# Layer 1 of a two-layer network: the state updated by one multiply-add on VectorE for each pair, the inverses begun three pieces later, and the quantised weight prepared behind the first block

## The chip, the core and the metric

The kernel runs on one NeuronCore of a Trainium2 chip. TensorE (PE) multiplies matrices, VectorE (DVE), ScalarE (ACT) and GpSimd (POOL) work on elements, and the transfers are issued from SyncE's queue (SP). The metric is device time of one launch in microseconds. Less is better. Three runs of the kernel before gave 3066.98, 3079.79 and 3086.23 us, so the median is 3079.79 us.

## What is computed

The input is one sequence of 4096 rows with 256 channels. Layer 0 (causal attention with 16 heads, then a mixture of experts) is not touched by the change. Layer 1 is a delta rule in chunks of 32 rows for 4 heads of 64 channels, followed by a multiplication with an int8 weight. Cut to what matters here, it computes:

```python
h = _layernorm(x) * (1 + ca) + sa
q, k, v = short_conv(h @ Wq, conv_q), short_conv(h @ Wk, conv_k), short_conv(h @ Wv, conv_v)
q, k = l2norm(rotary_mix(q)), l2norm(rotary_mix(k))
kb = k * beta[..., None]
gm = gamma.reshape(b, h, n, chunk).mean(-1)        # one number for a chunk and head
A = -(kb @ swapaxes(k, -1, -2)) * strict_lower      # 32 x 32 for each chunk and head
for i in range(1, chunk):                           # T = inverse of I - A
    A = A.at[..., i, :i].add(einsum('...j,...jc->...c', A[..., i, :i], A[..., :i, :i]))
T = A + eye(chunk)
u, w = T @ v, T @ kb

def step(S, xs):                                    # one chunk of 32 rows
    qi, ki, ui, wi, g = xs
    attn = qi @ swapaxes(ki, -1, -2) * tril_inc
    u_t = ui - wi @ S
    o_i = qi @ S + attn @ u_t
    S_new = g[..., None, None] * S + einsum('bhck,bhcv->bhkv', ki, u_t)
    return S_new, o_i
# ... o normed, times Wo, plus a gated mixer; x = x + ga * that
h = _layernorm(x) * (1 + cb) + sb
# round(h / scale) as int8 @ weight_q.T * scale * weight_scale + bias;  x = x + gb * that
```

The 128 steps of the scan follow each other: each needs the S of the one before.

## The kernel before

Layer 1 works on 8 blocks of 512 rows, each of four tiles of 128 rows. A tile has four chunks. `layer1` (from L1143) runs two streams of generators, `fronts` and `backs`. A piece is what a stream issues up to its next `yield`.

The front (`fronts`, L1266) norms and projects a block (`project`, nine pieces), and then for each tile convolves, rotates and normalises (`convolve`, `mix`), turns keys by channel (`keys_by_channel`) and builds the products of keys (`products`, L1555). `products` scales the products on ScalarE into a tile L, sends L and the betas to DRAM with four transfers each (L1576, L1578), and reads them back with two as Ls (L1581), where each partition has one 32 x 32 matrix. After a block's fourth tile, `solve` (L1585) starts the inverses of its 64 chunk and head pairs at once: GpSimd clears a tile T, ScalarE copies the diagonal from Ls (L1593), and VectorE then works through 31 columns with a multiply and a subtract each (`column`, L1603 and L1610). The last column sends T to DRAM and back as U (18 transfers). These columns are not issued at once. `begin` fills a list of them, and `solving(n)` hands out n of them wherever it is called.

The back (`backs`, L1639) runs the scan and what follows from it. `from_inverse` multiplies U with v and the keys into u and w, `scan` (L1677) does the four steps of a tile, and `weights`, `outputs` and ten further functions make the output of a tile, each a fixed number of pieces later. A step of the scan (L1683 to L1727) is: four TensorE products w @ S (eight matmul instructions) into the PSUM tile w (`pw`), two ScalarE operations that scale the old S by gm into a tile gs (L1694), four columns of an inverse, VectorE's ut = u - w @ S (L1699), one or two yields, TensorE's keys times ut into other columns of the same PSUM tile, three columns, and VectorE's S = gs + that (L1722). The PSUM tile has one buffer. A tile's `weights` hands out two more columns, so a tile takes 30 of the 31.

Three things set the order. First, `layer1` calls the streams: front alone, with three columns after each piece, until the first block's inverse has been issued (`alone(0)`), then `LEAD` = 18 front pieces, then 0.7 front pieces (`RATE`) for each back piece. Before a block's first `from_inverse`, `alone(b)` would run the front on if its inverse were missing. Second, `later(n, f)` has f issued n steps of its stream later (`stream`, L1185). A quiet f adds no piece. When a stream has ended, what waits is issued with no steps between, one piece for each f that is not quiet. Third, instructions issued through `self.mm`, `self.mma`, `self.tp` and `self.dv` (and `keep_in_program_order`) keep their order on their engine. ScalarE's and GpSimd's instructions and the transfers are not pinned: the framework orders those at compile time by what it takes to be ready. On each engine the final order is fixed, and an instruction that waits holds back all behind it.

In `layer1_weights` (L1209) the int8 weight is loaded as int32 words into a tile with gs's name, cast to bf16 on VectorE (L1252), transposed with four TensorE operations (L1257) and copied from PSUM by VectorE (L1260) into `wqT`. All of this is issued ahead of the first block's work. Its first use is `multiplied`, 17 pieces behind the first scanned tile.

Of the kernel before, what the change touches and what calls it, by code (L numbers as in the profile page):

```python
# [9 lines left out]
BF16 = mybir.dt.bfloat16  # L10
I8 = mybir.dt.int8
I32 = mybir.dt.int32
AF = mybir.ActivationFunctionType
ALU = mybir.AluOpType
# [3 lines left out]
P = 128  # L18
S = 4096
C = 256  # L20
# [76 lines left out]
class _Net:  # L97
# [1111 lines left out]
    def layer1_weights(self):  # L1209
        nc, a, wp = self.nc, self.a, self.wp  # L1210
        m = self.mods[1]
        w = self.w = {}
        w["masks"] = self.t(wp, [P, D_N], "masks")
        nc.sync.dma_start(out=w["masks"], in_=a["const_delta"])
        w["bg"] = self.t(wp, [P, 2, 9], "bg")
        for src, lo, hi in (("Wb", 0, 4), ("Wgamma", 4, 8), ("frac_gate_w", 8, 9)):
            nc.sync.dma_start(
                out=w["bg"][:, :, lo:hi], in_=a["L1_attn_" + src].rearrange("(k p) n -> p k n", p=P)
            )
        w["bgb"] = self.t(wp, [P, 9], "bgb")  # L1220
        nc.vector.memset(w["bgb"], 0.0)
        nc.sync.dma_start(out=w["bgb"][:, 8:9], in_=a["L1_attn_frac_gate_b"].partition_broadcast(P))

        w["ones"] = self.t(wp, [P, P], "ones")
        nc.gpsimd.memset(w["ones"], 1.0)


        rl = self.rows(wp, a["L1_attn_rot_logit"], 4, "rl")
        w["mix"] = self.t(wp, [P, 4], "mix")
        nc.scalar.activation(w["mix"], rl, AF.Sigmoid)  # L1230
        w["unmix"] = self.t(wp, [P, 4], "unmix")
        nc.vector.tensor_scalar(w["unmix"], w["mix"], -1.0, 1.0, ALU.mult, ALU.add)


        w["o"] = self.weight(wp, a["L1_attn_Wo"], C, "Wo")
        onw = self.t(wp, [P, 1], "onw")
        for half in range(2):
            nc.sync.dma_start(
                out=onw[64 * half : 64 * half + 64, :],
                in_=a["L1_attn_o_norm_w"].rearrange("(d o) -> d o", o=1),  # L1240
            )
        for k in range(2):
            nc.vector.tensor_scalar(w["o"][:, k, :], w["o"][:, k, :], onw, None, ALU.mult)
            nc.vector.tensor_tensor(w["o"][:, k, :], w["o"][:, k, :], m["ga"], ALU.mult)
        w["gmw"] = self.rows(wp, a["L1_attn_mixer_norm_w"], C, "gmw")
        nc.vector.tensor_tensor(w["gmw"], w["gmw"], m["ga"], ALU.mult)


        words = self.t(self.sp, [P, 2, C // 4], "gs", I32)
        nc.sync.dma_start(out=words, in_=a["L1_ffn_weight_q"].rearrange("(k p) n -> p k n", p=P))  # L1250
        wb = self.t(self.sp, [P, 2, C], "on", BF16)
        nc.vector.tensor_copy(wb, words[:, :, :].bitcast(I8))  # L1252
        w["qT"] = self.t(wp, [P, 2, C], "wqT", BF16)
        for k in range(2):
            ps = self.t(self.pf, [P, C], "f", BF16)
            for ok in range(2):
                nc.tensor.transpose(  # L1257
                    ps[:, ok * P : (ok + 1) * P], wb[:, ok, k * P : (k + 1) * P], self.identb
                )
            nc.vector.tensor_copy(w["qT"][:, k, :], ps)  # L1260
        w["wsg"] = self.rows(wp, a["L1_ffn_weight_scale"], C, "wsg")
        nc.vector.tensor_tensor(w["wsg"], w["wsg"], m["gb"], ALU.mult)
        w["bgo"] = self.rows(wp, a["L1_ffn_bias"], C, "bgo")
        nc.vector.tensor_tensor(w["bgo"], w["bgo"], m["gb"], ALU.mult)

    def fronts(self, later):  # L1266
        nc = self.nc
        for f in self.norm_block(0):
            f()
        yield from self.project(0, later)  # L1270
        for b in range(NB):
            more = b + 1 < NB
            for s in range(4):
                n = 4 * b + s
                parts = self.mix(b, s, later)
                for kinds in (("q", "k"), ("v",), ()):
                    if s in (0, 2):
                        for kind in kinds:
                            yield from self.convolve(s // 2, kind)
                    next(parts)  # L1280
                    yield None
                later(3, lambda n=n: self.keys_by_channel(n))
                later(4, lambda n=n: self.products(n, later))
                if s == 1 and more:
                    self.load_block(b + 1)
                    for at, f in zip((1, 3, 5, 7), self.norm_block(b + 1)):
                        later(at, f, quiet=True)
            if more:
                nc.gpsimd.tensor_copy(self.hT[:, :, 0:8], self.hT[:, :, 512:520])
                for rows in self.shifted:  # L1290
                    nc.gpsimd.tensor_copy(rows[:, :, :, 0:2], rows[:, :, :, 512:514])
                yield from self.project(b + 1, later)
# [292 lines left out]
    def solve(self, b, later):  # L1585


        nc, sp, Ls = self.nc, self.sp, self.Ls
        T = self.t(sp, [P, 16, 32], "T", bufs=1)
        nc.gpsimd.memset(T, 0.0)  # L1590
        for e in range(2):
            half = slice(64 * e, 64 * e + 64)
            nc.scalar.copy(  # L1593
                T[half].rearrange("p m r -> p (m r)")[:, e : e + 34 * 15 + 1 : 34],
                Ls[half].rearrange("p i j -> p (i j)")[:, 33 * e : 33 * e + 66 * 15 + 1 : 66],
            )

        def column(j):
            m, n = j // 2 + 1, 31 - j
            step = self.t(sp, [P, 16, 32], "step", bufs=1)  # L1600
            below = T[:, 0:m, j + 1 : 32]
            self.dv(
                nc.vector.tensor_tensor(  # L1603
                    step[:, 0:m, 0:n],
                    T[:, 0:m, j].unsqueeze(2).to_broadcast([P, m, n]),
                    Ls[:, j + 1 : 32, j].unsqueeze(1).to_broadcast([P, m, n]),
                    ALU.mult,
                )
            )
            self.dv(nc.vector.tensor_tensor(below, below, step[:, 0:m, 0:n], ALU.subtract))  # L1610

        def last():
            column(30)
            dU = self.t(self.dp, [4, 4, 4, 32, 32], "dU")
            for e in range(2):
                nc.sync.dma_start(
                    out=dU.rearrange("t c h (m e) r -> (t c h) m e r", e=2)[:, :, e, :],
                    in_=T[64 * e : 64 * e + 64],
                )
            for t in range(4):  # L1620
                for c in range(4):
                    at = slice(32 * c, 32 * c + 32)
                    nc.sync.dma_start(
                        out=self.U[(4 * b + t) % 6][at, :, at], in_=dU[t, c].rearrange("h j r -> j h r")
                    )
            self.solved += 1

        def begin():
            self.columns = [lambda j=j: column(j) for j in range(30)] + [last]

        later(4, begin, quiet=True)

    def solving(self, n=2):

# [42 lines left out]
    def scan(self, n, later):  # L1677

        nc, sp, kept = self.nc, self.sp, self.tiles[n]
        u, wT, gm = kept["u"], kept["w"], self.blocks[n // 4]["gm"][:, n % 4]  # L1680
        kept["states"] = []
        kept["ut"] = ut = self.t(sp, [P, 4, 64], "ut")
        for c in range(4):  # L1683
            rows = slice(32 * c, 32 * c + 32)
            state = self.state
            kept["states"].append(state)
            pw = self.t(self.pw, [P, 2, 512], "w")
            for pair in range(2):
                for par in range(2):
                    half = slice(64 * par, 64 * par + 64)  # L1690
                    self.mm(pw[rows, par, 64 * pair : 64 * pair + 64], wT[half, pair, rows], state[half, pair, :])
            gs = self.t(sp, [P, 2, 64], "gs")
            for pair in range(2):
                nc.scalar.activation(  # L1694
                    gs[:, pair, :], state[:, pair, :], AF.Identity, scale=gm[:, pair, c : c + 1]
                )
            self.solving(4)
            self.dv(
                nc.vector.tensor_tensor(  # L1699
# [11 lines left out]
            for pair in range(2):  # L1711
                for par in range(2):
# [5 lines left out]
                    )  # L1718
            self.state = self.t(sp, [P, 2, 64], "S", bufs=7)
            self.solving(3)  # L1720
            self.dv(
                nc.vector.tensor_tensor(  # L1722
                    self.state, gs, pw[:, 0, 128:256].rearrange("p (a d) -> p a d", d=64), ALU.add
                )
            )
            yield None

    def weights(self, n):
# [191 lines left out]
```

## Time and profile before

The profiled execution took 3067.4 us, and its span on the core is 3065.6 us; that is the low end of the three timed runs.

| What | Value |
|---|---|
| median of three runs | 3079.79 us |
| profiled execution, its span | 3067.4 us, 3065.6 us |
| granted TensorE clock, mean of the span | 0.912 |
| first loads of layer 1, first scan step | 2102, 2244 us |
| end of the front's matmuls | 2909 us |
| gs, 128x64 on ScalarE (L1694) | 256 times, 343 ns, 77.1 us |
| S, 128x128 on VectorE (L1722) | 128 times, 285 ns, 36.5 us |
| ut, 32x256 on VectorE (L1699) | 128 times, 416 ns, 53.3 us |
| columns, multiply and subtract (L1603, L1610) | 248 each, 315 and 272 ns |
| z, 128x256 multiply-multiply from PSUM on VectorE (L1873) | 32 times, 478 ns |

How to read the lines that follow in the prediction: a row of a timeline has the start and the duration in microseconds, the engine, the source line, the operation, the tile written and the tiles read, and in square brackets how long the engine was idle before it and which instruction ended that. L136, L1329 and L1338 are the helpers through which TensorE's work is issued, so the tile's name tells which it is: w is the scan's PSUM tile, f the front's and other PSUM tiles, o the output's. A row of windows has the window, then for each engine its busy time and number of instructions, and at the end the granted TensorE clock (1 is full speed), the share of the transfer engines and GB/s. A row of the list of waits has who waited for whom, the total in microseconds, how often, and the longest.

### The profile page before, as it was taken

The numbers are of one execution on the slowest core, as the hardware profiler recorded it, in microseconds if no ns is written. First come the engines' busy times: TensorE is split into PE (matmuls) and PEld (weight loads), VectorE is DVE, ScalarE is ACT, GpSimd is POOL, SyncE is SP. The second block draws the span as 40 slices with busy tenths as digits, with TensorE's granted clock in tenths as the row PEclk, the third lists the DMA queues.
The fourth block names the chain that finished last, engine by engine and source line by source line (L and its number), as shares of the span: only waits on it lengthen the run. The fifth ranks groups of instructions, "written<-read, shape, count | busy, mean of one in ns | idle before, by whom it ended". The sixth has DMA issues, their size and how long they took to land. (4 is left out here: it accounts for less than half of the span.)

```text
span 3065.6 us, 60519 instructions
## 1 busy us (share of the span) xinstructions
PE 2807.8 (92%) x24188; PEld 1603.6 (52%) x24188; DVE 2248.7 (73%) x3893; ACT 1814.6 (59%) x3831; POOL 473.1 (15%) x710
## 2 busy tenths in 40 slices
PE   7899999999999999999999899998688889889867
PEld 4454444444444444444444478886466566666545
DVE  6685988888888988989886266665447765765765
ACT  3335777777777787777888632223555455455411
POOL 3232000000000000000000121212324323333312
PEclk8897999999999999999999999998878877778855
DMA  5343000030000300001000100002221212112110
GB/s 187 134 178 66 12 12 7 12 53 7 12 12 7 53 7 12 12 19 38 7 2 2 40 27 28 21 15 80 37 37 27 47 37 43 30 43 41 18 18 11
DMA packets 175083, 111.23 MB, mean 36 GB/s; under 512 B 124177, under 2 KB 143377, under 8 KB 174225
## 3 DMA queue, kind: packets, MB, share of 16 engines
q1 hardware_dynamic: 174656, 107.28, 14.0%
q8 instruction: 191, 3.13, 0.4%
q14 instruction: 92, 0.75, 0.1%
q0 software_dynamic: 144, 0.07, 0.0%
HBM read 54.99 MB, written 37.81 MB: 30 GB/s over the span
## 5 line engine op out<-in xcount | busy, mean ns | idle before, releaser
L723 ACT ACTIVATE e<-e 128x512 f32<-128x512 f32 (+1 forms) x2176 | 1151.4, 583 | 318.7 <-PE e L136 285.1
L605 DVE TENSOR_REDUCE mx<-m 128x2 f32<-128x1024 f32 (+3 forms) x1088 | 1201.7, 1129 | 141.8 <-PE m L136 129.6
L136 PE MATMUL o<-e,vall 128*32 128x256 f32 (+2 forms) x9216 | 692.5, 375 | 6.2 <-ACT ot L700 5.4
L136 PE MATMUL e<-q,kt 50*128 50x512 f32 (+3 forms) x2688 | 573.0, 438 | 1.1 <-ACT e L723 1.0
L136 PE MATMUL m<-kt,q 48*128 48x512 f32 (+3 forms) x2688 | 478.0, 374 | 18.2 <-DVE mx L615 10.7
L136 PEld LDWEIGHTS e<-q,kt 50*128 50x128 f32 x2688 | 251.0, 185 | 433.4 <-issue 258.4
L136 PEld LDWEIGHTS o<-e,vall 128*32 128x32 f32 x9216 | 191.9, 108 | 325.8 <-issue 299.8
L136 PEld LDWEIGHTS m<-kt,q 48*128 48x128 f32 x2688 | 248.7, 189 | 91.9 <-issue 37.1
L1338 PE MATMUL b<-w,hid 128*128 128x512 f32 x768 | 198.0, 402 | 0.0
L902 POOL TENSOR_TENSOR full<-full,ga 128x512 f32<-128x512 f32 (+1 forms) x2 | 2.0, 1001 | 1115.1 <-DMA full<-in_L_attn_bo_dram 1102.8
L1127 DVE SCALAR_TENSOR_TENSOR x<-b,wd,x 128x256 f32<-128x256 f32 x256 | 123.5, 482 | 58.3 <-PE b L1338 51.3
L1338 PEld LDWEIGHTS b<-w,hid 128*128 128x128 f32 x768 | 143.9, 189 | 31.0 <-ACT hid L881 0.3
L1694 ACT ACTIVATE gs<-S,gm 128x64 f32<-128x64 f32 x256 | 77.1, 343 | 113.8 <-DVE S L1722 113.4
L136 PE MATMUL w<-S,uw 64*32 64x64 f32 x1024 | 66.8, 265 | 72.6 <-DVE S L1722 71.7
L1603 DVE TENSOR_TENSOR step<-T,Ls 128x126 f32<-128x126 f32 (+22 forms) x248 | 78.2, 315 | 70.8 <-ACT T L1593 32.8
L615 DVE TENSOR_REDUCE mx<-m 128x8 f32<-128x1024 f32 x64 | 78.4, 1225 | 64.0 <-PE m L136 63.7
L1699 DVE TENSOR_TENSOR ut<-uw,w 32x256 f32<-32x256 f32 x128 | 53.3, 416 | 84.1 <-PE w L136 82.6
L1338 PE MATMUL a<-hs,kt 128*128 128x512 f32 x384 | 104.0, 410 | 1.0 <-DVE hid L1077 1.0
L1722 DVE TENSOR_TENSOR S<-gs,w 128x128 f32<-128x128 f32 x128 | 36.5, 285 | 88.1 <-PE w L136 51.0
L136 PEld LDWEIGHTS w<-S,uw 64*32 64x32 f32 x1024 | 41.2, 129 | 113.3 <-DVE S L1722 95.8
L136 PE MATMUL w<-ut,kk 32*64 32x64 f32 x1024 | 69.8, 267 | 22.2 <-DVE ut L1699 22.1
L1338 PE MATMUL f<-hh,wqkv 128*128 128x512 f32 x288 | 87.4, 448 | 1.4 <-ACT rowsk L1373 0.9
(309 smaller groups left out, 3692.7 us busy)
## 6 DMA issues: line engine op xcount, KB each, us to landing
q<-qd SPq DMA_DIRECT2D x128, 96.0 KB
kt<-kd SPq DMA_DIRECT2D x12, 768.0 KB
kd<-high SPq DMA_DIRECT2D x32, 256.0 KB
qd<-high SPq DMA_DIRECT2D x32, 256.0 KB
x<-in_L_attn_x_dram SPq DMA_DIRECT2D x15, 512.0 KB
kd<-full SPq DMA_DIRECT2D x16, 256.0 KB
qd<-full SPq DMA_DIRECT2D x16, 256.0 KB
xd<-x SPq DMA_DIRECT2D x8, 512.0 KB
```

Of the source, the lines that this page charges most:

```text
L136: self.nc.tensor.matmul(out, lhsT, rhs, start=start, stop=True, skip_group_check=skip)
L605: nc.vector.tensor_reduce(mx[:, 2 * pair : 2 * pair + 2, s, col], ps[:, :, at : at + w], AX.X, ALU.max)
L615: nc.vector.tensor_reduce(mx[:, 2 * pair : 2 * pair + 2, :, 0], ps.rearrange("p h (s k) -> p h s k", k=P), AX.X, ALU.max,)
L723: nc.scalar.activation(e[:, 0:at], ps[:, 0:at], AF.Exp)
L902: nc.gpsimd.tensor_tensor(wide, wide, by.unsqueeze(1).to_broadcast([P, *shape]), op)
L1127: nc.vector.scalar_tensor_tensor(x, ps[:, e, :], wd[:, s, n : n + 1], x, ALU.mult, ALU.add)
L1338: self.nc.tensor.matmul(out, lhsT, rhs, start=(k == 0), stop=(k == n - 1))
L1603: nc.vector.tensor_tensor(step[:, 0:m, 0:n], T[:, 0:m, j].unsqueeze(2).to_broadcast([P, m, n]), Ls[:, j + 1 : 32, j].unsqueeze(1).to_broad ...
L1694: nc.scalar.activation(gs[:, pair, :], state[:, pair, :], AF.Identity, scale=gm[:, pair, c : c + 1])
L1699: nc.vector.tensor_tensor(ut[rows].rearrange("p (a b) d -> p a b d", b=2), u[rows].rearrange("p (a b) d -> p a b d", b=2), pw[rows, :, 0:1 ...
L1722: nc.vector.tensor_tensor(self.state, gs, pw[:, 0, 128:256].rearrange("p (a d) -> p a d", d=64), ALU.add)
```

## The change

The scaling on ScalarE and the tile gs are gone. The new S is made by two VectorE instructions, one for each pair of heads, as old S times gm plus the PSUM columns of the pair. `begin` is issued seven steps after `solve` in place of four. The quantised weight's load, cast, transposes and copies move out of `layer1_weights` into a function of their own, which the front calls behind the first block's projection; it is one front piece more. Its cast, transposes and copies are now pinned to program order, and its words lie in a tile with z's name.

```diff
@@ layer1_weights
-        words = self.t(self.sp, [P, 2, C // 4], "gs", I32)
-        nc.sync.dma_start(out=words, in_=a["L1_ffn_weight_q"].rearrange("(k p) n -> p k n", p=P))
-        wb = self.t(self.sp, [P, 2, C], "on", BF16)
-        nc.vector.tensor_copy(wb, words[:, :, :].bitcast(I8))
-        w["qT"] = self.t(wp, [P, 2, C], "wqT", BF16)
-        for k in range(2):
-            ps = self.t(self.pf, [P, C], "f", BF16)
-            for ok in range(2):
-                nc.tensor.transpose(
-                    ps[:, ok * P : (ok + 1) * P], wb[:, ok, k * P : (k + 1) * P], self.identb
-                )
-            nc.vector.tensor_copy(w["qT"][:, k, :], ps)
...
+    def quantised_weight(self):
+        nc, a, wp = self.nc, self.a, self.wp
+
+        words = self.t(self.sp, [P, 2, C // 4], "z", I32, bufs=1)
+        nc.sync.dma_start(out=words, in_=a["L1_ffn_weight_q"].rearrange("(k p) n -> p k n", p=P))
+        wb = self.t(self.sp, [P, 2, C], "on", BF16)
+        self.dv(nc.vector.tensor_copy(wb, words[:, :, :].bitcast(I8)))
+        self.w["qT"] = self.t(wp, [P, 2, C], "wqT", BF16)
+        for k in range(2):
+            ps = self.t(self.pf, [P, C], "f", BF16)
+            for ok in range(2):
+                self.tp(ps[:, ok * P : (ok + 1) * P], wb[:, ok, k * P : (k + 1) * P], self.identb)
+            self.dv(nc.vector.tensor_copy(self.w["qT"][:, k, :], ps))
...
@@ fronts
         yield from self.project(0, later)
+        self.quantised_weight()
+        yield None
...
@@ solve
-        later(4, begin, quiet=True)
+        later(7, begin, quiet=True)
...
@@ scan
-            gs = self.t(sp, [P, 2, 64], "gs")
-            for pair in range(2):
-                nc.scalar.activation(
-                    gs[:, pair, :], state[:, pair, :], AF.Identity, scale=gm[:, pair, c : c + 1]
-                )
...
             self.state = self.t(sp, [P, 2, 64], "S", bufs=7)
             self.solving(3)
-            self.dv(
-                nc.vector.tensor_tensor(
-                    self.state, gs, pw[:, 0, 128:256].rearrange("p (a d) -> p a d", d=64), ALU.add
-                )
-            )
+            for pair in range(2):
+                self.dv(
+                    nc.vector.scalar_tensor_tensor(
+                        self.state[:, pair, :],
+                        state[:, pair, :],
+                        gm[:, pair, c : c + 1],
+                        pw[:, 0, 128 + 64 * pair : 192 + 64 * pair],
+                        ALU.mult,
+                        ALU.add,
+                    )
+                )
             yield None
```

## The prediction

> **What bounds the kernel now.** I first read the page's header and its slices for the share of layer 1, then layer 1 in windows, then the timelines of VectorE and TensorE in one block, and the list of waits last, because it can name the wrong engine.
>
> ```profile
> span 3065.6 us, 60519 instructions
> PE 2807.8 (92%) x24188; PEld 1603.6 (52%) x24188; DVE 2248.7 (73%) x3893; ACT 1814.6 (59%) x3831; POOL 473.1 (15%) x710
> PEclk8897999999999999999999999998878877778855
> ```
>
> Layer 1 is the last 960 us: its first loads are issued at 2102 and the first scan step runs at 2244. The granted clock is already below 1 there. The windows below hold a whole block of 512 rows (blocks repeat every 112.8 us), then the stretch with the columns of an inverse, then the rest.
>
> ```profile
> 2382.50:2495.30 112.80, 96.37 (x909) 70.58 (x907) 73.71 (x204) 62.14 (x170) 37.13 (x69) 0.85 0.23 45
> 2489.80:2535.50 45.70, 35.10 (x302) 24.91 (x300) 36.70 (x109) 18.29 (x51) 12.84 (x27) 0.77 0.17 40
> 2535.50:2602.60 67.10, 62.25 (x564) 46.12 (x565) 36.54 (x95) 39.51 (x111) 24.01 (x41) 0.78 0.19 35
> ```
>
> In the rest TensorE is busy 62.25 of 67.1 us (93%) and bounds. In the column stretch it is idle 10.6 of 45.7 us, and VectorE bounds: it first stands still, then runs almost without a gap. VectorE there, then TensorE:
>
> ```profile
> 2486.70 0.29 DVE L1722 TENSOR_TENSOR S<-gs,w 128x128 f32<-128x128 f32 x1 [2.49 <-ACT rowsk L1373]
> 2489.40 0.43 DVE L1699 TENSOR_TENSOR ut<-uw,w 32x256 f32<-32x256 f32 x1 [2.42 <-PE w L136]
> 2495.32 0.21 DVE L1603 TENSOR_TENSOR step<-T,Ls 128x31 f32<-128x31 f32 x1 [5.49 <-ACT T L1593]
> 2496.86 0.29 DVE L1722 TENSOR_TENSOR S<-gs,w 128x128 f32<-128x128 f32 x1
> ```
>
> ```profile
> 2486.14 0.45 PE L136 MATMUL w<-ut,kk 32*64 32x64 f32 x8
> 2497.20 0.62 PE L136 MATMUL w<-S,uw 64*32 64x64 f32 x8 [2.66 <-DVE S L1722]
> 2505.88 0.32 PE L136 MATMUL w<-S,uw 64*32 64x64 f32 x2 [3.65 <-DVE S L1722]
> 2537.22 1.97 PE L136 MATMUL o<-ut,A 128*128 128x64 f32 x8
> 2564.95 1.10 PE L136 MATMUL o<-ut,A 128*128 128x64 f32 x8
> ```
>
> The first column waits 5.49 us for T, which ScalarE fills from Ls when that transfer lands. The scan's S is queued behind it, and TensorE waits for S.
>
> ```profile
> ACT gs L1694 <- DVE S L1722: 113.4, 63, 7.1
> DVE step L1603 <- ACT T L1593: 32.8, 6, 5.5
> DVE step L1603 <- DMA Ls<-dL: 32.0, 2, 19.7
> ```
>
> So six such stalls make 32.8 us, and the first and the last block have 19.7 and 12.3 us. The page also puts about 36 us of S's waits down to ScalarE. That is a trap: at 2486.70 the named rowsk has just ended, but so have the w matmuls that S reads (2486.14 + 0.45). Only 2.9 us (five times 0.58) are waits for gs itself. Taking gs away doesn't make S earlier.
>
> **The change, part by part.** The sum is against the profiled execution, 3067.4 us (span 3065.6). The median shown is 3079.8, 0.4% above it; I move the median by the same difference.
>
> *Inverses.* Counting yields in the code, `begin` (L1628) lands at the same place of the scan in blocks 1 to 6, before S of the last chunk of the block's second tile, because VectorE's columns are handed out by the scan. What moves is the front: the first scan step must await the first inverse, so all front work is three pieces (four with the quantised weight's) earlier against the scan. From `products` of a block's last tile to its `begin` there are then 13 pieces of the scan side, not 9. A block is 60 such pieces, 1.88 us each, so Ls is asked for 7.5 us earlier. That covers 5.5 us: 6 x 5.5 = **-33 us**. The front's transfers (24 of rows a block, ten for each `products`) move with it and keep their order on SP's queue; they pass only the scan's stores, one a tile. On GpSimd's queue the front's operations pass the scan's powers and adds, about 1 us each; GpSimd is busy 37.13 of 112.8 us, so I count nothing.
>
> What is late next is VectorE itself. At tile 11's first `ut`, just behind the last column, it has done the same front work in both orders, so the stall is gained whole there; but TensorE has 1.3 us less work in the stretch (keys and products 1.5, a convolution 1.1 come in; a projection 1.65 and two convolutions 2.2 go out), and has it in the rest, where it bounds: 6 x 1.3 = **+8 us**. In the last block `begin` follows `products` with no piece between, before and after, since the stream is drained there: the 12.3 us stay.
>
> In the first block `turning` comes after 9 columns, not 18. TensorE waits there 5.5 us for rot and 5.7 for kk, both behind columns; that shortens by some 6 us. The columns end some 4 us later (one more tile's rotation lies between), and with them U's transfers (16 issues, 8.4 us). TensorE reaches the first inverse's products 8.8 us after the last U is issued (2242.1, 2233.3), so I put this at **0**, between -6 and +6. The front's lead at the end is worth four pieces at the tail's pace in place of the block's, 15.6/15 = 1.04 against 1.88: **-3.4 us**.
>
> *State.* Out go 256 ScalarE scalings (343 ns, 77 us busy) and 128 adds of VectorE (128x128, 285 ns). In come 256 multiply-adds, 128x64, which no row shows. The nearest is z (L1873), also from PSUM with a scalar per row: 478 ns at 256 columns. S at 128 and ut at 256 columns (285, 416) give 1.02 ns a column, so at 64 columns 478 - 192 x 1.02 = 282 ns. How two follow each other:
>
> ```profile
> 2988.97 0.29 DVE L1722 TENSOR_TENSOR S<-gs,w 128x128 f32<-128x128 f32 x1 [0.40 <-PE w L136]
> 2989.17 0.16 DVE L1848 RECIPROCAL rq<-xs 128x1 f32<-128x1 f32 x1
> ```
>
> The next starts 0.20 us after S. The pair takes 0.20 + 0.28 = 0.48 us against 0.285: **+0.2 us** a chunk. The Trainium skill, "VectorE: DVE Perf Modes", the section on the errata, speaks against this edit: each instruction pays its fixed price, so many small tiles pay it many times. Its formula for an fp32 tensor_tensor, (N + 151)/0.96 ns, gives 291 at 128 (the row says 285) and 224 at 64: +0.16 a chunk. I take the trace's 0.2. The bounds are 0.1 and, if nothing shrinks with width, 2 x 0.478 - 0.085 - 0.285 = 0.6.
>
> No overlap of the halves helps: tile w has one buffer, so the next chunk's matmuls wait for both. Where TensorE has other matmuls to do after a chunk (half a microsecond and more), 0.2 is hidden. It shows in the column stretch (5 chunks a block) and where TensorE waits for S in the rest (3 a block): 8 x 6 x 0.2 = 9.6 us. In the tail 2.5 chunks of each of nine tiles are on the chain: 4.5 us. Sum **+14 us**; if the cover were gone everywhere, 128 x 0.2 = 26 us.
>
> ScalarE waits at gs for S 113 us, but the operations behind it (convk, on, uw at 2502, 2509 and 2517) wait for TensorE anyway. I credit one wait, TensorE for mixer (1.35 us a block at 2532.5), with the 0.6 us that one pair of gs takes: **-3.6 us**.
>
> *Quantised weight.*
>
> ```profile
> 2109.29 2.07 ACT L1322 ACTIVATE nxn<-x,nnm,nrs 128x256 f32<-128x256 f32 x4
> 2112.65 0.59 PE L1257 MATMUL f<-identb,on 128*128 128x128 bf16 x4 [10.59 <-DMA bgo<-in_L_ffn_bias_dram]
> 2113.03 1.91 PE L1329 MATMUL f<-k,nxn 128*128 128x128 f32 x8
> ```
>
> nxn is complete at 2111.4, but its transposes are queued behind the weight's until 2113.0: -1.6 us. The four transposes come back behind the projection: +0.6. The cast (0.43 us) and two copies (0.28 each) fall in VectorE's 15 us wait for qk (2119 to 2134). **-1.0 us.** That supposes the transfer to be issued early. It has no input to wait for, and the table trig, also written behind the projection's first pieces, is issued at 2109.6. SP's queue then loses one issue (0.39 us) ahead of wsg and bgo. Were it issued behind the rows at 2131.5 (3.7 us from issue to cast), the first convolution on TensorE and `turning` on VectorE would queue behind it: +7 us.
>
> Sum: -33 + 8 + 0 - 3.4 + 14 - 3.6 - 1 = **-19 us**: 3048 for the profiled execution, 3061 as a median.
>
> **The rivals.** *TensorE's clock stays up* (0.32). Fewer gaps may spare half-speed stretches. The trace: after the stall's window (TensorE busy 0.76 of 3.42 us) the clock is 0.5 most of the time to 2521, and again from 2535 to 2555, where `o<-ut,A` takes 1.97 us against 1.10. The Trainium skill, "TensorE: Matmul & The Clock Gate", part 1, says that about 3.4 us of idleness halve the clock; here gaps of 2.66 and 1.35 us were enough, so by the rule only the stall counts and by the trace smaller gaps do too. The stretch at 2535 lies where TensorE bounds and costs 20 x (1 - 1.10/1.97) = about 9 us. If half to all of the six blocks lose it: -19 - 27 to -54, 3034 to 3007. Against it: the gaps of the column stretch remain, and one of them can throttle as before.
>
> *The pair is dear* (0.10; the other side). At 0.6 us a pair the 70 exposed chunks cost 41 us, not 14, and the 58 others are no longer covered by half a microsecond of TensorE; with half of those, +17. Sum -19 + 27 + 17 = +25, and with all 128 exposed, -33 + 77 = +44: 3105 to 3124. It decides from 33/128 = 0.26 us a pair if all are exposed, 0.47 if 70 are. For it: S is the loop's own chain, and VectorE has no gap in the column stretch. Against: ut and S do shrink with width.
>
> *The stall only changes its name* (0.08). `turning` reaches VectorE's queue nine columns earlier and may wait for qk, and the weight's transfer may come late: -19 + 15 + 7 = +3, 3083.
>
> **How the numbers follow.** My sum has 0.50; with its bounds (first block 6 us either way, S 7 us less or 12 more, the stall's cover a few us) it spans 3045 to 3076. One per cent, about what a measurement of this kernel can tell from no change, is 3049 to 3111. Faster by more: the clock's case and the low end of mine (0.08), 0.40. Slower by more: most of the dear pair, 0.08. Within: 0.52. The range leaves out the clock's best end and the dear pair: 3020 to 3090.
>
> **What would show it.** Right: the first column in blocks 1 to 6 waits under 1 us for T; the last block still about 12; blocks under 110 us; multiply-adds of about 0.28 us, 0.48 a pair; S still named as waiting for TensorE; the nxn transposes start at once behind nxn. Wrong: a column stretch as long as before with another wait in it, pairs of 0.6 us and more, or half-clock windows that come or go.

## The result, and the profile after

The changed kernel takes 3092.9 us (median of 20 runs) against 3077.8 us for the kernel before, timed beside it: ratio 1.0052, interval 1.0033 to 1.0072. It is half a per cent slower. Forecast were 3061 us in a range of 3020 to 3090, with slower by over 1% at 0.08; the direction was wrong, and the time lies just above the range. Medians are over all runs and ratios over the fast runs alone, so a ratio is not always that of two medians.

The page of the changed kernel: the span, the busy times, and the granted clock in 40 slices.

```profile
span 3101.1 us, 60445 instructions
PE 2824.2 (91%) x24188; PEld 1616.5 (52%) x24188; DVE 2268.9 (73%) x4021; ACT 1750.2 (56%) x3575; POOL 472.5 (15%) x710
PEclk8895999999999999999999899998888878778855
```

Not all of the 35.5 us between the two spans belongs to the change. Layer 0 is the same in both programs, yet the first load of layer 1 is issued at 2115.41 us here and at 2102.13 before. So I measure layer 1 from that issue to the end of the span: 963.5 us before, 985.7 after, **+22.2 us**. All "layer 1" times below are taken so, from one profiled execution each. Two kernels were profiled twice, and their layer 1 differs by 0.8 us (e4, e12) and 3.3 us (e7, e13), while its first load comes anywhere from 2101 to 2146 us in the 14 traces. ScalarE lost 64 us of work, VectorE gained 20, and the layer became longer.

The windows are the third block, from its first column to the fourth's, and then the fourth in two parts: from the start of its first column's wait the stretch with the columns, and the rest up to the next wait (length, busy time and instructions of PE, PEld, DVE, ACT and POOL, then granted clock, transfer share, GB/s).

```profile
2409.45:2522.50 113.05, 93.85 (x862) 70.02 (x862) 75.80 (x220) 50.05 (x130) 36.40 (x68) 0.80 0.19 37
2516.90:2562.60 45.70, 32.48 (x254) 24.43 (x250) 34.68 (x106) 12.18 (x35) 11.39 (x23) 0.73 0.09 21
2562.60:2629.20 66.60, 60.34 (x612) 44.40 (x612) 41.13 (x113) 37.76 (x95) 25.27 (x45) 0.90 0.26 49
```

The two blocks take 113.0 and 112.3 us. Before, the same two took 105.9 and 112.8:

```profile
2389.41:2495.32 105.91, 90.24 (x862) 67.05 (x862) 73.28 (x203) 57.40 (x162) 36.94 (x68) 0.84 0.20 40
2495.32:2608.14 112.82, 97.36 (x862) 71.05 (x862) 73.26 (x204) 57.81 (x162) 36.85 (x68) 0.77 0.19 37
```

So the kernel before has two kinds of block. Its 862 matmul instructions, with the same stall of 5.49 us, take 90.2 us of TensorE at a granted clock of 0.84 and 97.4 us at 0.77. The 112.8 us that the prediction takes for every block is of the longer kind: from the second block's first column to the seventh's the intervals are 105.0, 105.9, 112.8, 113.1 and 109.4 us before, and 110.7, 113.0, 112.3, 112.9 and 112.8 after.

Where the 22.2 us lie: up to the third block's first column layer 1 takes 294.0 us (287.3 before), from there to the last block's first column 538.9 (533.4), from there to the end 152.8 (142.9). The gain expected of the blocks is missing, and all three parts are longer. VectorE's timeline shows why: the wait of the first column is still there.

```profile
2513.71 0.47 DVE L1721 SCALAR_TENSOR_TENSOR S<-S,gm,w 128x64 f32<-128x64 f32 x2 [2.52 <-PE w L136]
2516.45 0.43 DVE L1697 TENSOR_TENSOR ut<-uw,w 32x256 f32<-32x256 f32 x1 [2.27 <-PE w L136]
2522.49 0.21 DVE L1606 TENSOR_TENSOR step<-T,Ls 128x31 f32<-128x31 f32 x1 [5.61 <-ACT T L1596]
2524.27 0.47 DVE L1721 SCALAR_TENSOR_TENSOR S<-S,gm,w 128x64 f32<-128x64 f32 x2
```

And the list of waits over the span has the two rows of the first column as before, hardly changed (32.8 and 32.0 us there). TensorE's wait for S is longer (71.7 us there):

```profile
PE w L136 <- DVE S L1721: 86.9, 41, 4.9
DVE step L1606 <- ACT T L1596: 33.3, 6, 5.6
DVE step L1606 <- DMA Ls<-dL: 30.1, 2, 19.5
```

Yet Ls is asked for earlier. Its two transfers are issued from 2511.79, 5.1 us ahead of the wait's start; before, from 2488.81, 1.0 us ahead. The reason is in ScalarE's timeline, which shows its queue in order; first before, then after:

```profile
2494.59 0.60 ACT L1432 ACTIVATE convq<-f 128x512 f32<-128x512 f32 x1 [0.99 <-PE f L136]
2495.08 0.45 ACT L1593 COPY T<-Ls 64x16 f32<-64x16 f32 x2
```

```profile
2515.47 1.28 ACT L1435 ACT_TABLE_LOAD   x1
2516.76 0.60 ACT L1435 ACTIVATE convq<-f 128x512 f32<-128x512 f32 x1
2519.18 0.60 ACT L1435 ACTIVATE convk<-f 128x512 f32<-128x512 f32 x1 [1.82 <-PE f L136]
2520.74 0.58 ACT L1451 COPY qk<-f 128x512 f32<-128x512 f32 x1 [0.97 <-PE f L1332]
2521.36 0.98 ACT L1460 ACTIVATE rot<-qk,unmix 128x128 f32<-128x128 f32 x3
2522.25 0.20 ACT L1596 COPY T<-Ls 64x16 f32<-64x16 f32 x1
2522.36 0.40 ACT L1460 ACTIVATE rot<-qk,unmix 128x128 f32<-128x128 f32 x1
2522.78 0.22 ACT L1596 COPY T<-Ls 64x16 f32<-64x16 f32 x1
```

The two copies that fill T now stand behind both convolutions, the copy qk and the rotations of the next block, which themselves wait for TensorE. Before, they stood directly behind convq. Nobody wrote this order: these instructions aren't pinned. The chain that ended last agrees; between 2516 and 2530 us it runs over the front's matmuls, qk and rot to T's copies, the columns and S, and no transfer is in it. Some of its pieces (start, duration, what):

```profile
2518.12 1.01 PE f L136 x8
2519.13 1.06 PE f L1341 x4
2520.19 0.45 PE f L1332 x4
2520.74 0.59 ACT qk L1451
2521.67 0.68 ACT rot L1460 x2
2522.78 0.23 ACT T L1596
2524.27 0.47 DVE S L1721 x2
```

So two theories had to be told apart. *Queue*: the change is slow because T's copies slid back in ScalarE's queue. *Pair*: the two multiply-adds lengthen the chain of S by more than the sum allowed for.

### The profile page after: what moved, and what is told of

Read it like the earlier page. It is cut to its first block, busy times and chain, and to the rows that moved or that the text cites. A ratio compares the mean times of both kernels' runs of the same rounds, so it can differ in the third digit from the quotient of the medians.

```text
span 3101.1 us, 60445 instructions
## 1 busy us (share of the span) xinstructions
PE 2824.2 (91%) x24188; PEld 1616.5 (52%) x24188; DVE 2268.9 (73%) x4021; ACT 1750.2 (56%) x3575; POOL 472.5 (15%) x710
## 4 chain that ended last, share of the span: by engine, by line
PE 65%; DVE 24%; ACT 5%; issue 3%; POOL 2%; DMA 1%; SPq 0%; DVEq 0%; ACTq 0%; POOLq 0%
PE o L136 16%; PE e L136 13%; DVE mx L605 9%; PE m L136 8%; PE b L1341 6%; PE f L1341 5%; PE f L136 5%; PE a L1341 4%; PE w L136 3%; DVE step L1606 2%; DVE T L1613 2%; PE ps L1341 2%; ACT e L723 1%; PE f L1332 1%; DVE S L1721 1%
## 5 line engine op out<-in xcount | busy, mean ns | idle before, releaser
L136 PE MATMUL m<-kt,q 48*128 48x512 f32 (+3 forms) x2688 | 480.9, 376 | 15.3 <-DVE mx L615 9.0
L1606 DVE TENSOR_TENSOR step<-T,Ls 128x126 f32<-128x126 f32 (+22 forms) x248 | 78.5, 317 | 69.5 <-ACT T L1596 33.3
L1721 DVE SCALAR_TENSOR_TENSOR S<-S,gm,w 128x64 f32<-128x64 f32 x256 | 60.2, 276 | 87.7 <-PE w L136 86.1
L136 PE MATMUL f<-frac,hT 128*128 128x128 f32 x640 | 94.9, 304 | 0.0
```

The source lines that it names most:

```text
L136: self.nc.tensor.matmul(out, lhsT, rhs, start=start, stop=True, skip_group_check=skip)
L1606: nc.vector.tensor_tensor(step[:, 0:m, 0:n], T[:, 0:m, j].unsqueeze(2).to_broadcast([P, m, n]), Ls[:, j + 1 : 32, j].unsqueeze(1).to_broad ...
L1721: nc.vector.scalar_tensor_tensor(self.state[:, pair, :], state[:, pair, :], gm[:, pair, c : c + 1], pw[:, 0, 128 + 64 * pair : 192 + 64 * ...
```

## The experiments

Each kernel was timed in five rounds against the kernel before, and its ratio is to that: median 3081.0 us beside e1 to e4, 3076.7 beside e5 and e7 to e9, 3071.0 beside e10 to e13, each group on one chip. The last column is the total wait of the first columns for T's copies on ScalarE, by the list of waits; where VectorE makes the copies there is no such wait. The first block (19 to 20 us) and the last (10 to 12 us), which wait for Ls itself, are not in it.

| Kernel | begin | new state | T's copies by | median, us | ratio, interval | layer 1, us | wait for T |
|---|---|---|---|---|---|---|---|
| before | 4 | add | ScalarE | 3077.8 | 1 | 963.5 | 32.8 |
| changed | 7 | pair | ScalarE | 3092.9 | 1.0052, 1.0033 to 1.0072 | 985.7 | 33.3 |
| e1 | 4 | pair | ScalarE | 3105.6 | 1.0094, 1.0066 to 1.0123 | 984.2 | 32.8 |
| e2 | 7 | add | ScalarE | 3061.6 | 0.9963, 0.9939 to 0.9987 | 948.2 | 8.7 |
| e3 | 7 | add | ScalarE | 3063.1 | 0.994, 0.9918 to 0.9962 | 948.1 | 8.7 |
| e4 | 7 | pair | VectorE | 3062.8 | 1.0004, 0.9971 to 1.0037 | 950.7 | |
| e5 | 4 | add | VectorE | 3064.4 | 0.9936, 0.9903 to 0.997 | 941.6 | |
| e7 | 7 | add | VectorE | 3051.9 | 0.9915, 0.988 to 0.9949 | 937.5 | |
| e8 | 7 | pair, scalings kept | ScalarE | 3098.0 | 1.0063, 1.0029 to 1.0097 | 983.3 | 33.2 |
| e9 | 7 | two adds | ScalarE | 3073.9 | 0.9965, 0.9925 to 1.0004 | 956.3 | 8.7 |
| e10 | 4 | pair | VectorE | 3084.1 | 1.0027, 0.9998 to 1.0056 | 972.2 | |
| e11 | 7 | pair | ScalarE, placed | 3057.7 | 0.9956, 0.992 to 0.9992 | 944.4 | none |
| e12 (e4 again) | 7 | pair | VectorE | 3058.1 | 0.9956, 0.9936 to 0.9977 | 951.5 | |
| e13 (e7 again) | 7 | add | VectorE | 3042.6 | 0.9895, 0.9869 to 0.9921 | 934.2 | |

e1, e2, e5 and e10 have the old place of the quantised weight, the others the new one.

### One part at a time: e1 to e4

e1 is the kernel before with the scan's part of the diff alone, e2 the kernel before with the later begin, e3 the changed kernel with that part undone, e4 the changed kernel with T's copies moved.

```diff
 e2, in solve of the kernel before
-        later(4, begin, quiet=True)
+        later(7, begin, quiet=True)
 e4, in solve of the changed kernel (the two nc.scalar.copy above column go away)
         def begin():
+            for e in range(2):
+                half = slice(64 * e, 64 * e + 64)
+                self.dv(nc.vector.tensor_copy(T[half]..., Ls[half]...))
             self.columns = [lambda j=j: column(j) for j in range(30)] + [last]
```

> The kernel before with the new state alone (two multiply-adds on VectorE, no gs on ScalarE); begin at 4, quantised weight where it was. Theory A (the pair is what costs: 0.19 us more on the loop's chain for each of 128 chunks): slower than before by 8 to 24 us, ratio 1.003 to 1.008, and more time of TensorE waiting for S (72 us before, some 105 in the changed kernel). Theory B (the later begin costs, since it brings more front work of VectorE into the stretch of the columns): within 4 us of before.

> The kernel before with begin at 7 alone. Theory A: within 5 us of before; the stall ahead of the first column stays about 5.5 us in six blocks, because the copies of T's diagonal stand behind later convolutions and rotations in ScalarE's queue. Theory B: slower by 8 to 20 us, most of it in the first two blocks, as in the changed kernel. If the stall is gone here (under 1 us), the place of T's copies depends on gs, and both theories need mending.

> The changed kernel with the old state (gs on ScalarE, one add of 128x128): begin at 7 and the moved weight remain. Theory A: 8 to 24 us faster than the changed kernel, so 0.997 to 1.002 of before. Theory B: as the changed kernel, 1.003 to 1.007 of before.

> The changed kernel, with T's diagonal copied by VectorE just ahead of the first column instead of by ScalarE (two small copies a block). Theory A (ScalarE's queue makes the stall): the wait ahead of the first column falls from 5.6 to under 0.6 us in six blocks, those of the first and last block stay; VectorE's stretch shortens and the kernel is 12 to 33 us faster than the changed kernel, 0.993 to 1.001 of before. Rival C (blocks keep their 112.8 us whatever is taken out, since something else sets the period, such as TensorE's clock): stall gone, time within 5 us of the changed kernel.

Measured: the state alone costs 20.7 us of layer 1, and the six stalls stay. This isn't the price of the pair alone. From the second block's first column to the seventh's, e1's intervals are 105.8, 116.4, 115.1, 106.8 and 115.1 us, at granted clocks of 0.85 and 0.86 in the two short ones and 0.77 to 0.78 in the long. TensorE's listed wait for S did not rise as expected: 68.3 us, with 16.0 more put down to rq, the instruction behind S (71.7 before).

The later begin alone gains 15.3 us; its stalls fall to 0.7 us in five of six blocks, as the list of waits of e2 shows (total, times, longest; one of the five stands under another name):

```profile
DVE step L1603 <- ACT T L1593: 8.0, 5, 5.3
```

So the later begin does what it should, as long as the state is the old one. That was the third outcome named for e2, under which both theories needed mending, and e3 gained more over the changed kernel (37.6 us of layer 1) than either foresaw. e3 against e2 gives the place of the quantised weight: 948.1 against 948.2, nothing. The edits don't add up: -15.3 and +20.7 would give +5.4, and the changed kernel has +22.2. In e4, with T's copies at a fixed place on VectorE, the same two edits give 950.7 us, and the first column no longer waits in blocks 1 to 6 (0.03 us). Its ratio and its medians didn't agree well, and it was timed again as e12, with 0.9956.

### Is it the missing work of ScalarE? e8, and the split add e9

e8 puts the scalings back into the changed kernel, though nothing reads them. e9 keeps the scalings and the old arithmetic, and splits the add.

```diff
 e8, in scan of the changed kernel
+            gs = self.t(sp, [P, 2, 64], "gs")
+            for pair in range(2):
+                nc.scalar.activation(gs[:, pair, :], state[:, pair, :], AF.Identity, scale=gm[:, pair, c : c + 1])
             self.solving(4)
 e9, in scan of e3
-            self.dv(nc.vector.tensor_tensor(self.state, gs, pw[:, 0, 128:256]..., ALU.add))
+            for pair in range(2):
+                self.dv(nc.vector.tensor_tensor(self.state[:, pair, :], gs[:, pair, :],
+                    pw[:, 0, 128 + 64 * pair : 192 + 64 * pair], ALU.add))
```

> The changed kernel with the two ScalarE scalings of the old state put back where they were, though nothing reads them: the multiply-adds of VectorE, begin at 7 and the weight stay. It only restores ScalarE's load and, as the queue theory has it, the order of ScalarE's queue. Queue theory: T's copies stand ahead of the convolutions and rotations again, the first column of blocks 2 to 6 waits about 0.7 us in place of 5.6 to 6, and layer 1 takes 948 to 956 us (changed kernel 985.7), ratio 0.994 to 0.997. Pair theory (the multiply-adds are what costs): layer 1 stays at 975 us or more, ratio above 1.002.

> The changed kernel with the old ScalarE scalings, and the add split into two of 128x64: as many VectorE instructions for a new state as the changed kernel has, each a little shorter or as long, with ScalarE's queue as in the old state. Against the same kernel with one add of 128x128 (layer 1 948.1 us, ratio 0.994). Pair theory, 0.2 us more for each of 128 chunks on the chain: up to 26 us more, 974 us, ratio 1.002. My own count of 70 exposed chunks: 14 us more, 962 us. Queue theory alone, with the pair hidden: 948 to 953 us, ratio 0.994 to 0.996.

e8 went against my expectation: 983.3 us, and stalls of 5.6 us. Its ScalarE timeline has T in the same bad place though the scalings are back:

```profile
2395.05 0.58 ACT L1451 COPY qk<-f 128x512 f32<-128x512 f32 x1 [0.95 <-PE f L1332]
2395.66 0.98 ACT L1460 ACTIVATE rot<-qk,unmix 128x128 f32<-128x128 f32 x3
2396.55 0.20 ACT L1596 COPY T<-Ls 64x16 f32<-64x16 f32 x1
```

So it isn't the absence of the scalings that moves T back. The form of the state is what differs: with begin at 7 and one add or two (e3, e9) T stands well, with the multiply-adds it doesn't; with begin at 4 (e1) they leave it behind convq as before. How the framework comes to that order wasn't traced further. e8 also shows that taking 77 us of work off ScalarE was worth nothing here (983.3 with it, 985.7 without).

### Is it T's place in the queue, or the arrival of Ls? e5 and e11

e5 moves T's copies to VectorE in the kernel before, with begin at 4. e11 leaves them on ScalarE in the changed kernel, and only has the closing activations of the convolutions issued behind them.

```diff
 e11, in convolve of the changed kernel (self.filled is T's last copy; self.solves is 0 up to the first block's solve)
-                nc.scalar.activation(out, ps, AF.Silu)
+                if self.solves:
+                    with self.tc.issue_after(self.filled.ins):
+                        nc.scalar.activation(out, ps, AF.Silu)
+                else:
+                    nc.scalar.activation(out, ps, AF.Silu)
```

> The kernel before with one thing changed: the two diagonal copies of Ls into T are made by VectorE at the head of begin (begin still at 4, old state, old weight). In the kernel before, the last Ls transfer is issued at 2489.8 us and ScalarE makes the copies at 2495.08, right behind convq. Queue theory (a good part of the stall is T's copies standing behind other ScalarE work): the first column's wait, 5.49 us in blocks 1 to 6, falls to about 3 us, and layer 1 (963.5 us from its first load to its end) shortens by 10 to 16 us, to 947 to 953; ratio about 0.996. Arrival theory (the transfer of Ls is late and nothing else): VectorE waits for Ls as long as it waited for T, 5 us and more; layer 1 963 us; ratio 1.000.

> The changed kernel with one constraint: ScalarE's activations that close a convolution are issued behind the two copies that fill T for the inverse last prepared. The copies stay on ScalarE and every operation is the changed kernel's; only their place in ScalarE's queue moves. Queue theory: the first column of blocks 1 to 6 waits under 1.5 us in place of 5.6, and layer 1 takes 948 to 960 us, near the 950.7 us with the copies on VectorE. Rival (it is VectorE's making the copies, or less load of ScalarE, that helped, or Ls lands too late for either): the wait stays above 4 us and layer 1 above 975 us.

e11 decides for the queue: 944.4 us in place of 985.7, with every operation of the changed kernel on its old engine. ScalarE's timeline, then VectorE's:

```profile
2504.84 0.55 ACT L1602 COPY T<-Ls 64x16 f32<-64x16 f32 x2
2505.41 1.28 ACT L1438 ACT_TABLE_LOAD   x1
2506.71 0.60 ACT L1438 ACTIVATE convq<-f 128x512 f32<-128x512 f32 x1
2508.67 0.60 ACT L1438 ACTIVATE convk<-f 128x512 f32<-128x512 f32 x1 [1.36 <-PE f L136]
```

```profile
2505.94 0.43 DVE L1703 TENSOR_TENSOR ut<-uw,w 32x256 f32<-32x256 f32 x1 [2.27 <-PE w L136]
2506.40 0.21 DVE L1612 TENSOR_TENSOR step<-T,Ls 128x31 f32<-128x31 f32 x1
```

T is filled before the table load, and the column runs directly behind ut. Of the 41.3 us, 33.3 are the stall itself. With it the granted clock from the third block's first column to the last's rises from 0.81 to 0.86; whether that is the other 8 us was not separated.

e5 shows that even in the kernel before the queue had a part in the stall. The wait of VectorE in one block, now for the transfer itself:

```profile
2418.75 0.18 DVE L1625 COPY T<-Ls 64x16 f32<-64x16 f32 x1 [1.82 <-DMA Ls<-dL]
2419.19 0.18 DVE L1625 COPY T<-Ls 64x16 f32<-64x16 f32 x1 [0.26 <-DMA rowsv<-rowsv]
2419.40 0.21 DVE L1596 TENSOR_TENSOR step<-T,Ls 128x31 f32<-128x31 f32 x1
```

About 2.1 us of waiting in place of 5.5, and 12.8 us in blocks 1 to 6 in place of 32.8; layer 1 gains 21.9 us, more than expected. Here the copies run 3.2 us after the issue of Ls (2415.58), before 6.3 us after it.

### What does the pair cost by itself? e7, e10, e12, e13

All have T's copies on VectorE by the edit of e4, so T's place doesn't move. e7 and e13 are that edit on e3, e12 is e4 again, and e10 is that edit on e1.

> The changed kernel with the old state (two ScalarE scalings, one add) and T's copies on VectorE; begin at 7, weight behind the first block. Beside the kernel with the new state and T's copies on VectorE (layer 1 950.7 us) it shows the price of the pair where no stall is left. If the pair itself is dear (0.28 us a chunk on the chain of S, 128 chunks): 915 to 930 us, ratio about 0.985. If the pair's price is mostly hidden or balanced, and what made the change slow was T's place in ScalarE's queue: 944 to 951 us, ratio about 0.994. First column's wait below 0.5 us in blocks 1 to 6 under both.

> The kernel before with the new state and T's copies on VectorE; begin at 4, old weight. It fills the last place of the table of begin (4 or 7), state (old or new) and the engine of T's copies. With the old state the same kernel took 941.6 us in layer 1; with begin at 7 the pair cost 13.2 us (950.7 against 937.5). If the pair has a price of its own that does not depend on the stall, 953 to 957 us here, ratio about 0.998. If the pair's price is set by how the framework orders the rest (with T's copies on ScalarE and begin at 4 it was 20.7 us), 960 us and more, ratio above 1.000.

> The changed kernel with T's copies on VectorE a second time, beside the same with the old state on the same chip, since its first ratio (1.0004) and its first medians (3062.8 against 3081.0) do not agree. Layer 1 again 948 to 953 us. Against its neighbour the pair's price in device time: 13 us, 0.4%, if the profiled 13.2 us of layer 1 are the price; up to 36 us if all 128 chunks pay the 0.28 us.

> The changed kernel with the old state and T's copies on VectorE a second time, as the partner of the run before it: layer 1 935 to 940 us, ratio 0.988 to 0.995, some 13 us below its partner.

With begin at 7 the pair costs 13.2 us of layer 1 (e4 against e7) and 17.3 (e12 against e13), between the two outcomes put down for e7; the medians of the last two, on one chip, are 15.5 us apart. On the chain of S it is dearer than its duration. VectorE's S and TensorE's next matmul, in e13 (one add) and e12 (pair):

```profile
2507.67 0.28 DVE L1726 TENSOR_TENSOR S<-gs,w 128x128 f32<-128x128 f32 x1
```

```profile
2508.01 0.32 PE L136 MATMUL w<-S,uw 64*32 64x64 f32 x2 [5.00 <-DVE S L1726]
```

```profile
2504.31 0.47 DVE L1722 SCALAR_TENSOR_TENSOR S<-S,gm,w 128x64 f32<-128x64 f32 x2
```

```profile
2504.92 0.32 PE L136 MATMUL w<-S,uw 64*32 64x64 f32 x2 [5.12 <-DVE S L1722]
```

From the start of S to TensorE's start it is 0.34 us with one add and 0.61 with the pair, 0.27 more. Counted in the traces, TensorE stands idle until S and starts at these distances in 57 of the 128 chunks of e13 and 63 of e12, and 63 times 0.27 is 17 us. With e9's two adds the distance is 0.50 us, in 58 chunks: 58 times 0.16 gives 9.3 us, and measured are 956.3 - 948.1 = 8.2, again between the outcomes put down.

With begin at 4 the pair costs more, 30.6 us (e10 against e5). That is the second of the outcomes put down for e10, but most of it is not VectorE's. Between the gap before TensorE's matmuls of mixer and the scores of the next tile, both kernels do the same 209 matmul instructions; first e5, then e10:

```profile
2566.76:2587.11 20.35, 18.61 (x209) 12.24 (x209) 14.91 (x42) 11.67 (x37) 9.41 (x16) 0.92 0.15 24
```

```profile
2542.08:2571.10 29.02, 27.35 (x209) 17.77 (x209) 15.52 (x45) 9.26 (x28) 9.22 (x16) 0.59 0.10 15
```

In e10 TensorE runs there at a granted clock of 0.59 in place of 0.92, and takes 8.7 us longer. Over the starts of ut, this stretch takes 8.7, 7.3 and 6.4 us longer in three of the blocks: 22 of the 30.6 us. The gap ahead of it is 1.67 us in e10 and 1.35 in e5. Neither that gap nor the pair decides the clock there. The kernel before has the gap of 1.35 us in six blocks, and the granted clock over the 20 us behind it is 1.00, 1.00, 0.56, 0.55, 0.57 and 0.91. Two of these stretches:

```profile
2426.54:2446.54 20.00, 17.66 (x216) 11.96 (x216) 15.30 (x44) 12.16 (x38) 9.40 (x16) 1.00 0.16 24
2532.52:2552.52 20.00, 19.30 (x154) 12.91 (x156) 10.43 (x33) 8.32 (x25) 6.17 (x12) 0.56 0.14 22
```

e1, with the pair and the gap of 1.67 us, has 0.91, 0.51, 0.50, 0.91, 0.50 and 0.91. So the 22 us are no price of the pair that could be counted on, and some 8 are left for it.

## Why the prediction was wrong

**The stall (-33 us): this step failed.** The prediction put it as "Ls is asked for 7.5 us earlier. That covers 5.5 us: 6 x 5.5 = -33 us", and took T to be filled "from Ls when that transfer lands". It listed what an earlier front brings to SP's, GpSimd's and VectorE's queues, but for ScalarE only the work that goes, not the order of what stays. The text before it says that ScalarE's instructions aren't pinned; so a change of the state could reorder them, and it did. The lead grew by 4.1 us, not 7.5 (1.0 to 5.1 in the block shown, 1.3 to 5.5 on average of the six); that was enough, as e11 shows with the same begin, but T's copies were no longer next. Even of the old 5.5 us, only some 2 were the transfer (e5).

**Without that, the sum holds.** e11 is the changed kernel with T in place: 944.4 - 963.5 = -19.1 us, where the sum was -19; with the copies on VectorE it is -12.8 and -12.0. The ratios of e11 and e12 are both 0.9956. That is partly luck, term by term:

- *Carried work and lead* (+8, 0, -3.4): with begin alone (e2) 24.1 us of stall go and 15.3 us are gained, so 8.8 us come back, where these terms give 4.6. One block, the second, kept its stall (5.26 us), which the prediction didn't foresee.
- *State* (+14): 13 to 17 with begin at 7. The total was about right, its factors were not: 0.27 us at some 60 chunks, not 0.2 at 70. The multiply-adds themselves are as predicted, 276 ns, 0.47 for the pair.
- *ScalarE's relief* (-3.6): nothing (e8, in which the stall remains).
- *Quantised weight* (-1.0): nothing measurable (e3 against e2).

For the changed kernel itself these sizes add up to about what it lost: no stall gone (0.5 us more), 8.8 for the carried work, 13 to 17 for the pair, 22 to 26 us against the 22.2 of layer 1. That the carried work costs as much there as in e2 is an estimate.

**The rivals.** "The pair is dear" gave a slower kernel, but through 0.6 us more a chunk; VectorE needs 0.19 us more, and TensorE starts 0.27 later. "The stall only changes its name" is nearest in kind, but the prediction looked for a new wait on VectorE, and the old one stayed under its old name. "TensorE's clock stays up" did not come, as the stall that it builds on stayed: from the third block's first column to the last block's the granted clock is 0.81 after and 0.79 before. In e11 and e13, without stalls, it is 0.86 there, so this rival had something right; how much of a gain is the clock's was not separated. Its reading that a gap of 1.35 us was enough to halve the clock does not hold: the same gap is followed by a full clock in two blocks of the same trace.

**The signs named.** "The first column in blocks 1 to 6 waits under 1 us for T" was the right place to look, and says wrong: 5.6 us. "Blocks under 110 us" could tell little, since three of the five intervals above were under 110 us in the kernel before; after, none is. The nxn transposes do start behind nxn without a wait for the weight. The last block's wait for Ls is 10.6 us where about 12 was expected.

## What to carry to other kernels

Where a framework orders an engine's unpinned instructions, an edit on another engine can move the one that a critical wait hangs on; before counting a stall as gone, ask which instruction ends it, what can be ordered ahead of it, and fix its place. Of a wait with a transfer and a small copy behind it, look at how long after the transfer's issue the copy runs: here more than half of the stall, 3.4 of 5.5 us, was the copy's place. Before taking one block for all, measure several: here equal blocks of one execution differ by 7 us with the granted clock. The fastest kernel of the study, e13, keeps the one add, begins later and fills T at a fixed place: 0.9895 (0.9869 to 0.9921) of the kernel before.

## What the runs showed of the hardware

- Splitting an operation cost the waiting engine here more than the second instruction. TensorE starts 0.06 us after the end of one add (0.34 - 0.28), but 0.14 to 0.15 after the end of a pair, whether of multiply-adds (0.61 - 0.47) or adds (0.50 - 0.35).
- An add of 128x64 takes 215 ns on VectorE (the prediction has 224 as a second estimate) and a multiply-add with a scalar per row 276; an add of 128x128 takes 285. Half the width saves a quarter of the add, and the multiply-add spends it.
- The same 209 matmul instructions took 18.6 or 27.4 us of TensorE at granted clocks of 0.92 and 0.59. The length of the idle gap ahead does not decide which: behind gaps of 1.35 us in one execution the clock over 20 us was 1.00, 0.91 or 0.55 to 0.57.
- In all 14 traces the granted clock is either 0.5 or 1, and it changes only at multiples of 3.41 us from its first change. Where a gap lies between them differs from block to block; that this decides is not shown.
